# Group norm statistics made one layer early, and a convolution shared out anew between TensorE and VectorE

## The chip, the cores and the metric

The kernel runs on one core of one Trainium2 chip. The metric is device time in microseconds, from one execution's start to its end; a time of the kernel is the median of several executions. The profile is of one further execution, with its own time. Engines are written as in the profile: PE (TensorE), PEld (its weight loads), DVE (VectorE), ACT (ScalarE), POOL (GpSimd), SP (the queue that issues all DMAs here).

## The reference

Four images of 64 x 64 pixels with 192 channels pass through four layers. Each layer is a residual block: group norm over 32 groups of 6 channels and all pixels, then a state space model, added to its input.

```python
def _gn(v, G=32, eps=1e-5):
    B_, H_, W_, C_ = v.shape
    g = v.reshape(B_, H_, W_, G, C_ // G)
    m = jnp.mean(g, axis=(1, 2, 4), keepdims=True)
    s = jnp.var(g, axis=(1, 2, 4), keepdims=True)
    return ((g - m) / jnp.sqrt(s + eps)).reshape(v.shape)

x = x + _L0_conv_ref(_gn(x), ...)   # a: four directions, rows and columns, 4-tap convolution along each, 384 channels
x = x + _L1_conv_ref(_gn(x), ...)   # b: 3x3 depthwise convolution, one snake-wise direction, 384 channels
x = x + _L2_conv_ref(_gn(x), ...)   # c: 3x3 depthwise convolution, four directions, 192 channels
x = x + _L3_conv_ref(_gn(x), ...)   # d: as c, 384 channels
```

Inside a layer (here b), with 16 states per channel:

```python
xc, z = jnp.split(x @ in_proj_w.T, 2, axis=-1)
xc = silu(conv(xc) + conv_b)
dts, Bs, Cs = split(x_proj_w @ xc)
delta = softplus(dt_w @ dts + dt_b)
h[t] = exp(delta[t] * A) * h[t-1] + delta[t] * xc[t] * B[t]     # along the direction
y[t] = sum over states of h[t] * C[t]  +  D * xc[t]
y = layer_norm(y) * silu(z)                                     # a: without the layer norm
out = y @ out_proj_w.T
```

## The kernel before

`net` (L936) goes image by image and layer by layer. An image of a layer is 192 channels by 4096 pixels, kept as two halves (`k`) of 96 partitions; between layers it lies in DRAM, and a layer writes it in eight chunks of 512 pixels (8 image rows). Every layer has three stages, each with its own pools of tiles in SBUF and PSUM (`p1`, `p2`, `p3`).

**First stage (p1).** `load_x` (L65) reads the layer's input in four DMAs of 1024 pixels. `stats` (L83) sums all pixels on DVE (L87), multiplies the sums with `gmat` on PE to get the group's mean (L89), squares the distances on ACT in eight pieces with accumulated sums (L99), and makes the reciprocal root from a second small matmul (L106) with `rsqrt` (L72: Ln and Exp on ACT, then a Newton step on DVE). `normalize` (L113) then writes x in place in two instructions of 96x4096.

For b, c and d, `conv` (L123) follows. The inner channels are `nb` blocks of `P` (three of 128; in c two of 96). The weights `wu` and the taps `cp` are issued on SP at L130 and L132, after x. For each block, in the order 1, 2, 0, there are eight projections into PSUM (`pu`, L150, two matmuls each; the profile shows two records for each matmul) and eight copies by ACT into the padded image `pad` (L154). Blocks other than 0 are convolved on DVE: nine taps, one instruction each over the whole block of 4096 elements (L160 the first, L162 the other eight), then a silu on ACT (L137; in b two instructions, L138 and L139, since odd rows are turned round). Block 0 is convolved on PE: for each of eight chunks nine matmuls with a diagonal matrix of taps (`diag` L168, `pc` L177), and a silu.

For a, `conv1d` (L185) is called for each of four directions, with three blocks each: projections (L210), copies (L214), four taps on DVE (L238 and L240), silu (L241) into `xo`, and a DMA of `xo` to DRAM (L242). Block 0's first 16 rows (`CONV_ROWS`) go by PE (L232, L233) instead. `pad` has four buffers, `xo` two.

**Scans (p2).** `scans` (L269) handles tiles of 128x1024: decays by ACT, inflow on POOL or as transposes on PE, the scan on DVE, outflow on DVE or POOL, sums on PE. The order on each engine is written out by hand: `keep` (L256) ties every instruction to the one before it on its engine. In layer a (`short`) the start of each row must not carry a state over, so some decays are written into three fixed tiles that POOL sets to zero beforehand (L293), leaving each row's first column alone.

**Output (p3).** `output` (L680) reads the directions' results in eight chunks, adds them, makes layer norm statistics per pixel (L705, L706), gates by silu of a second projection; then for eight chunks it normalizes (L727), transposes (L734), scales (L744), multiplies (L745), projects (L752), adds the layer's input (`gy`, L747) into `res` on DVE (L756, once per half) and stores it (L757). Layer a has `out0` (L802), whose `finish` (L836) does the same last steps at L839 and L842.

**Order.** Outside the scans a planner in the language's framework orders each engine's instructions when the kernel is built, by program order and by when it thinks their inputs are ready. In the profile, `dg` (L168) runs before the mean is copied (L91), for example, and taps of two blocks take turns on DVE. Engines then work through their lists in order. `behind` (L56) forces a few places. A new stage's pools take over the memory of the old one's: in the profile, the first load and the first memset of a first stage begin when the last store of the stage ahead has landed.

Of the kernel before, what the change touches and what calls it, by code (L numbers as in the profile page):

```python
# [7 lines left out]
F32 = mybir.dt.float32  # L8
AF = mybir.ActivationFunctionType
ALU = mybir.AluOpType  # L10
# [17 lines left out]
CONV_ROWS = 16  # L28
POOL_SHORT = 5, 8
# [15 lines left out]
class Net:  # L45
    def __init__(self, tc, d, const):
        self.tc, self.nc, self.d = tc, tc.nc, d
        self.pinned = {}
        nc = self.nc
        self.ident = const.tile([128, 128], F32, tag="ident", name="ident")  # L50
        make_identity(nc, self.ident)
        self.gmat = const.tile([HP, HP], F32, tag="gmat", name="gmat")
        nc.sync.dma_start(self.gmat, d["gmat"])
# [11 lines left out]
    def load_x(self, pool, x_src, key):  # L65
        x = pool.tile([HP, 2, L], F32, tag="x", name=f"x_{key}")
        for q in range(4):
            s = slice(q * (L // 4), (q + 1) * (L // 4))
            self.nc.sync.dma_start(x[:, :, s], x_src[:, :, s])
        return x  # L70
# [12 lines left out]
    def stats(self, keep, pool, pp, x, key):  # L83

        nc = self.nc
        sums = pool.tile([HP, 2], F32, tag="sums", name=f"sums_{key}")
        nc.vector.tensor_reduce(sums, x, AX.X, ALU.add)  # L87
        ps = pp.tile([HP, 2], F32, tag="gps", bufs=1, name=f"gm_{key}")
        nc.tensor.matmul(ps, self.gmat, sums, start=True, stop=True)  # L89
        mean = keep.tile([HP, 2], F32, tag="mean", name=f"mean_{key}")  # L90
        nc.vector.tensor_copy(mean, ps)  # L91
        neg = pool.tile([HP, 2], F32, tag="neg", name=f"neg_{key}")
        nc.vector.tensor_scalar(neg, mean, -1.0, None, ALU.mult)
        part = pool.tile([HP, 2, 4], F32, tag="part", name=f"part_{key}")
        for k in range(2):
            for q in range(4):
                n = L // 4
                junk = pool.tile([HP, n], F32, tag="junk", bufs=2, name=f"junk_{key}{k}{q}")
                nc.scalar.activation(  # L99
                    junk, x[:, k, q * n : (q + 1) * n], AF.Square, bias=neg[:, k : k + 1],  # L100
                    accum_out=part[:, k, q : q + 1],
                )
        sq = pool.tile([HP, 2], F32, tag="sums", name=f"sq_{key}")
        nc.vector.tensor_reduce(sq, part, AX.X, ALU.add)
        ps = pp.tile([HP, 2], F32, tag="gps", bufs=1, name=f"gv_{key}")
        nc.tensor.matmul(ps, self.gmat, sq, start=True, stop=True)  # L106
# [4 lines left out]
        return mean, rstd  # L111

# [10 lines left out]
    def conv(self, pool, pp, xn, xc, sums, P, nb, w_u, cpack, taps, shape, interior, borders, snake, key):  # L123
# [16 lines left out]


        done = []
        for b in [*range(1, nb), 0]:
# [11 lines left out]
            if b:  # L155
                acc = img(sums[:, b, :])
                for i, (tr, tcol) in enumerate(taps):
                    v = pad[:, tr : tr + H, tcol : tcol + W]
                    if i == 0:
                        nc.vector.tensor_scalar(acc, v, cp[:, b, :1], None, ALU.mult)  # L160
                    else:
                        nc.vector.scalar_tensor_tensor(  # L162
                            acc, v, cp[:, b, i : i + 1], acc, ALU.mult, ALU.add
                        )
                done.append(silu(img(xc[:, b, :]), acc, b))
                continue
# [7 lines left out]
            for ch in range(NCH):  # L174
# [10 lines left out]
    def conv1d(self, pool, pp, xn, out, w_u, cpack, cols, rev, key):  # L185
# [10 lines left out]
        for b in range(nb):  # L196
# [37 lines left out]
            a = img(acc)[:, r0:, :]  # L234
            for i, t in enumerate(taps):
                v = pad[:, t + r0 : t + H, :] if cols else pad[:, r0:, t : t + W]
                if i == 0:
                    nc.vector.tensor_scalar(a, v, cp[:, b, :1], None, ALU.mult)  # L238
                else:
                    nc.vector.scalar_tensor_tensor(a, v, cp[:, b, i : i + 1], a, ALU.mult, ALU.add)  # L240
            done.append(nc.scalar.activation(to[:, r0:, :], a, AF.Silu, bias=bias))  # L241
# [27 lines left out]
    def scans(self, sp, pp, dp, xc, P, nb, dirs, short):  # L269
# [16 lines left out]
        if short:  # L286
# [3 lines left out]
            fixed = []  # L290
            for k in range(3):
                f = sp.tile([P, NT, T], F32, tag=f"dAs{k}", bufs=1, name=f"dAs{k}_{dirs[0][3]}")
                keep(nc.gpsimd.memset(f, 0.0))  # L293
                fixed.append(f)
# [205 lines left out]
        def decay(t):  # L500
# [3 lines left out]
            elif short:  # L504
                t.dA = fixed[t.turn % 3]
# [174 lines left out]
    def output(self, pool, pp, P, nb, outs, wz, wo, ln, snake, x_src, norm, dst, key):  # L680
# [8 lines left out]
        for ch in range(NCH):  # L689
# [21 lines left out]
            for b in range(nb):  # L711
# [5 lines left out]
                gates.append(nc.scalar.activation(z[:, b, s], pz, AF.Silu))  # L717
        v = pool.tile([128, NCH * TB, 1], F32, tag="v", name=f"v_{key}")
# [4 lines left out]
        for ch in range(NCH):  # L723
# [33 lines left out]
            nc.sync.dma_start(dst[:, :, s], res)  # L757

    def layer0(self, x_src, dst, dp):
        tc, nc, d = self.tc, self.nc, self.d
        P, nb = 128, 3
        with tc.tile_pool(name="a_keep", bufs=1) as keep:
            jobs = []
            with tc.tile_pool(name="a_p1", bufs=1) as pool, tc.tile_pool(
                name="a_p1ps", bufs=1, space=PSUM
            ) as pp:
                x = self.load_x(pool, x_src, "a")
                nc.scalar.preload_act_table_set(NLE)  # L770
                norm = self.stats(keep, pool, pp, x, "a")
                self.normalize(x, x, norm)
# [24 lines left out]
            with tc.tile_pool(name="a_p3", bufs=1) as pool, tc.tile_pool(  # L797
                name="a_p3ps", bufs=1, space=PSUM
            ) as pp:
                self.out0(pool, pp, x_src, norm, [j[4] for j in jobs], dst)  # L800

    def out0(self, pool, pp, x_src, norm, outs, dst):  # L802
# [32 lines left out]

        def finish(ch, x, po):  # L836
# [5 lines left out]
            nc.sync.dma_start(dst[:, :, ch * T : (ch + 1) * T], res)  # L842

# [34 lines left out]
        finish(late[0], late[4], late[3])  # L878

    def layer(self, name, x_src, dst, dp, P, nb, dirs, snake, twice):  # L880
# [5 lines left out]
        with tc.tile_pool(name=f"{name}_keep", bufs=1) as keep:  # L886
            with tc.tile_pool(name=f"{name}_xc", bufs=1) as xp:
                xc = xp.tile([P, nb, L], F32, tag="xc", name=f"xc_{name}")
                with tc.tile_pool(name=f"{name}_p1", bufs=1) as pool, tc.tile_pool(
# [3 lines left out]
                    x = self.load_x(pool, x_src, name)  # L893
                    nc.scalar.preload_act_table_set(NLE)
                    norm = self.stats(keep, pool, pp, x, name)
# [133 lines left out]
```

## Time and profile before

| | us |
|---|---|
| median of 3 runs | 35065.01 (35061.34 to 35067.1) |
| the profiled execution | 35048.62 |
| its span, first to last instruction | 35046.5 |

| engine | busy us | share of the span |
|---|---|---|
| PE | 25072.0 | 72% |
| PEld | 18264.5 | 52% |
| DVE | 27941.2 | 80% |
| ACT | 23687.5 | 68% |
| POOL | 25888.4 | 74% |

DMA moved 98 GB/s over the span; the mean granted clock of PE was 0.810. The four images take nearly the same time each (a, b, c and d in turn): the second image's layer a begins to load at 8759.65 us.

A line of a timeline gives start, duration, engine, line of the code, operation, what it writes and reads, shapes, the count, and in brackets how long the engine stood idle before and what released it. A line of waits gives who waited, for whom, then the sum in us, how often, and the longest. "Idle before" matters only on the engine that is late.

### The profile page before, as it was taken

Reading aid. Unit: us, or ns where it says so; the run is one execution under the profiler, and the core shown is the slowest. Engines: PE = TensorE matmul, PEld = TensorE weight load, DVE = VectorE, ACT = ScalarE, POOL = GpSimd, SP = SyncE. Lnnn points to the kernel's source line nnn. Section 1 sums busy time; section 2 is a strip of 40 time slices with the busy share of each in tenths; the row PEclk is TensorE's granted clock in tenths of the full one; section 3 lists DMA queues with packets and bytes.
Section 4 is the critical chain, followed back from the end, with each engine's and each line's share of the span. In section 5 each row is a group of like instructions: output and inputs, shape, how many; then the busy total and the mean of one; then the engine's idle time right before and its main releaser. Section 6 shows DMA issues by size and latency. Waiting matters only on the chain. (4 is left out here: it accounts for less than half of the span.)

```text
span 35046.5 us, 390536 instructions
## 1 busy us (share of the span) xinstructions
PE 25072.0 (72%) x135744; PEld 18264.5 (52%) x135744; DVE 27941.2 (80%) x22892; ACT 23687.5 (68%) x44483; POOL 25888.4 (74%) x11298
## 2 busy tenths in 40 slices
PE   7778777766777877776677787777667778777766
PEld 4554454554455445455445544545544554454554
DVE  7885797887788579788778857978877885797887
ACT  6773585776677358577667735857766773585776
POOL 6882696887588269688758826968876882696887
PEclk8888777878888887788888888778788888777878
DMA  3332233223333223322333322332233332233223
GB/s 107 106 106 76 85 106 98 94 94 110 107 106 106 75 86 106 98 93 93 111 106 106 107 75 86 108 97 94 94 111 106 106 106 76 85 106 98 94 94 111
DMA packets 1370822, 3443.13 MB, mean 98 GB/s; under 512 B 183201, under 2 KB 630545, under 8 KB 1362705
## 3 DMA queue, kind: packets, MB, share of 16 engines
q1 hardware_dynamic: 1368848, 3418.15, 31.1%
q8 instruction: 1076, 17.63, 0.2%
q14 instruction: 898, 7.35, 0.1%
HBM read 2962.60 MB, written 455.08 MB: 98 GB/s over the span
## 5 line engine op out<-in xcount | busy, mean ns | idle before, releaser
L595 PE MATMUL py_d<-ident,c_d 128*128 128x128 f32 x24576 | 3815.0, 314 | 2143.3 <-POOL c_d L577 1313.4
L595 PE MATMUL py_a<-ident,c_a 128*128 128x128 f32 x24576 | 3630.7, 302 | 2217.6 <-POOL c_a L577 1149.3
L577 POOL TENSOR_TENSOR c_d<-h_d,C_d 128x1024 f32<-128x1024 f32 x2036 | 4779.0, 2368 | 162.5 <-DVE h_d L560 159.9
L577 POOL TENSOR_TENSOR c_a<-h_a,C_a 128x1024 f32<-128x1024 f32 x1908 | 4479.4, 2371 | 414.8 <-issue 281.3
L595 PEld LDWEIGHTS py_d<-ident,c_d 128*128 128x128 f32 x24576 | 3359.8, 164 | 2596.2 <-POOL c_d L577 1633.4
L595 PEld LDWEIGHTS py_a<-ident,c_a 128*128 128x128 f32 x24576 | 3150.5, 156 | 2527.0 <-DVE c_a L577 1267.2
L522 POOL TENSOR_TENSOR u_d<-du_d,B_d 128x1024 f32<-128x1024 f32 x1536 | 3621.5, 2362 | 899.9 <-issue 886.7
L522 POOL TENSOR_TENSOR u_a<-du_a,B_a 128x1024 f32<-128x1024 f32 x1536 | 3607.4, 2364 | 715.0 <-DVE h_a L553 695.3
L577 POOL TENSOR_TENSOR c_c<-h_c,C_c 96x1024 f32<-96x1024 f32 x1356 | 3179.0, 2361 | 365.4 <-DVE h_c L560 346.2
L560 DVE TENSOR_TENSOR_SCAN h_d<-dA_d,carry_d,u_d 128x512 f32<-128x512 f32 x2536 | 3073.4, 1264 | 334.8 <-POOL c_d L577 264.3
L514 ACT ACTIVATE dA_d<-delta_d,A_d 128x512 f32<-128x512 f32 x3072 | 2118.0, 690 | 1637.0 <-DVE c_d L577 1491.6
L514 ACT ACTIVATE dA_a<-delta_a,A_a 128x512 f32<-128x512 f32 x3072 | 2119.6, 690 | 1243.0 <-DVE c_a L577 1089.6
L595 PE MATMUL py_c<-ident,c_c 96*128 96x96 f32 x16384 | 2232.5, 303 | 865.3 <-DVE c_c L577 653.7
L553 DVE TENSOR_TENSOR_SCAN h_a<-dA_a,u_a 128x1024 f32<-128x1024 f32 x1140 | 2579.4, 2281 | 331.2 <-ACT dA_a L518 178.3
L595 PEld LDWEIGHTS py_c<-ident,c_c 96*128 96x128 f32 x16384 | 2022.9, 180 | 1200.2 <-DVE c_c L577 779.3
L522 POOL TENSOR_TENSOR u_c<-du_c,B_c 96x1024 f32<-96x1024 f32 x1024 | 2412.8, 2362 | 6.3 <-DVE dA_c L560 6.0
L539 PE MATMUL ut_d<-ident,dut_d 128*128 128x128 f32 x12288 | 1911.8, 307 | 620.7 <-DVE c_d L577 595.3
L531 ACT ACTIVATE dut_a<-duT_a,BT_a 128x384 f32<-128x384 f32 x4096 | 2291.2, 604 | 0.0
L531 ACT ACTIVATE dut_d<-duT_d,BT_d 128x384 f32<-128x384 f32 x4096 | 2290.8, 601 | 0.0
L560 DVE TENSOR_TENSOR_SCAN ut_d<-dAs_d,carry_d,ut_d 128x512 f32<-128x512 f32 x1536 | 1971.1, 1283 | 388.3 <-issue 166.8
L514 ACT ACTIVATE dAs_d<-delta_d,A_d 128x512 f32<-128x512 f32 x3072 | 2042.9, 713 | 295.7 <-DVE h_d L560 230.5
L539 PEld LDWEIGHTS ut_d<-ident,dut_d 128*128 128x128 f32 x12288 | 1587.0, 158 | 1141.8 <-issue 934.9
(356 smaller groups left out, 63171.0 us busy)
## 6 DMA issues: line engine op xcount, KB each, us to landing
C_a<-bc_a SPq DMA_DIRECT2D x1024, 512.0 KB
C_d<-bc_d SPq DMA_DIRECT2D x1024, 512.0 KB
C_c<-bc_c SPq DMA_DIRECT2D x1024, 384.0 KB
B_a<-bc_a SPq DMA_DIRECT2D x512, 512.0 KB
B_d<-bc_d SPq DMA_DIRECT2D x512, 512.0 KB
B_c<-bc_c SPq DMA_DIRECT2D x512, 384.0 KB
C_b<-bc_b SPq DMA_DIRECT2D x256, 512.0 KB
xd_a<-xo_a SPq DMA_DIRECT2D x48, 2048.0 KB
```

The costliest lines, as they stand in the source:

```text
L514: keep(nc.scalar.activation(out, delta, AF.Exp, scale=o.A[:, t.b, k : k + 1]))
L522: keep(nc.gpsimd.tensor_tensor(t.u, t.c.du[:, t.b, None, :].to_broadcast([P, NT, T]), t.c.B[t.j], ALU.mult))
L531: keep(nc.scalar.activation(c.scaled[n][:, q, :], c.duT[:, q, :], AF.Copy, scale=c.BT[:, q, n : n + 1]))
L539: keep(nc.tensor.transpose(t.u[:, n, q * 128 : (q + 1) * 128], t.c.scaled[t.n0 + n][:, q, t.b * P : (t.b + 1) * P], self.ident,))
L553: keep(nc.vector.tensor_tensor_scan(hf, af, uf, 0.0, ALU.mult, ALU.add))
L560: keep(nc.vector.tensor_tensor_scan(hf, af, uf, o.carry[:, t.b, k : k + 1], ALU.mult, ALU.add))
L577: keep(engine.tensor_tensor(t.cm, t.h, t.c.C[t.j], ALU.mult))
L595: keep(nc.tensor.matmul(c.py[b][:, q, :], t.cm[:, n, q * 128 : (q + 1) * 128], self.ident[:P, :P], start=first, stop=c.sums[b] == NS and q ...
```

## The change

1. `moments` makes the statistics of one chunk with `bn_stats`, two instructions per chunk (one for each half), in the output stage: after each chunk's `res` is made, from `res`. In layer d the next input is the next image, so each chunk of it is loaded (`nx`) and read there; after the last image there is none, and `res` is read. The first image's statistics are made ahead of everything from eight loads of their own.
2. `stats` starts from those: `bn_aggr` for each half, mean by a matmul with `gmat`, then each channel's variance plus its squared distance from the group's mean, and a second matmul.
3. `load_normal` loads x in eight DMAs of 512 pixels, and normalizes in sixteen instructions of 96x512.
4. In `conv`, blocks other than 0 are convolved on DVE in two parts (31 and 33 rows; in b 30 and 34), each with its own silu. Block 0's last two chunks (in c its last three) go from PE to DVE.
5. In `conv1d`, DVE's taps and the silu are made in two parts, parted at row 37.
6. Layer a's scans have three fixed tiles for each of the two senses of direction (six memsets for three).

```diff
+CONV_SPLIT = 37
...
-    def load_x(self, pool, x_src, key):
-        x = pool.tile([HP, 2, L], F32, tag="x", name=f"x_{key}")
-        for q in range(4):
-            s = slice(q * (L // 4), (q + 1) * (L // 4))
-            self.nc.sync.dma_start(x[:, :, s], x_src[:, :, s])
-        return x
+    def moments(self, st, x, ch):
+
+        for k in range(2):
+            self.nc.vector.bn_stats(st[:, k, ch, :], x[:, k, :])
+
+    def new_moments(self, key):
+        return self.const.tile([HP, 2, NCH, 6], F32, tag="mom", bufs=2, name=f"mom_{key}")
...
-    def stats(self, keep, pool, pp, x, key):
+    def stats(self, keep, pool, pp, st, key):
 
         nc = self.nc
-        sums = pool.tile([HP, 2], F32, tag="sums", name=f"sums_{key}")
-        nc.vector.tensor_reduce(sums, x, AX.X, ALU.add)
+        mv = pool.tile([HP, 2, 2], F32, tag="gmv", name=f"gmv_{key}")
+        for k in range(2):
+            nc.vector.bn_aggr(mv[:, k, :], st[:, k, :, :])
         ps = pp.tile([HP, 2], F32, tag="gps", bufs=1, name=f"gm_{key}")
-        nc.tensor.matmul(ps, self.gmat, sums, start=True, stop=True)
+        nc.tensor.matmul(ps, self.gmat, mv[:, :, 0], start=True, stop=True)
         mean = keep.tile([HP, 2], F32, tag="mean", name=f"mean_{key}")
         nc.vector.tensor_copy(mean, ps)
-        neg = pool.tile([HP, 2], F32, tag="neg", name=f"neg_{key}")
-        nc.vector.tensor_scalar(neg, mean, -1.0, None, ALU.mult)
-        part = pool.tile([HP, 2, 4], F32, tag="part", name=f"part_{key}")
-        for k in range(2):
-            for q in range(4):
-                n = L // 4
-                junk = pool.tile([HP, n], F32, tag="junk", bufs=2, name=f"junk_{key}{k}{q}")
-                nc.scalar.activation(
-                    junk, x[:, k, q * n : (q + 1) * n], AF.Square, bias=neg[:, k : k + 1],
-                    accum_out=part[:, k, q : q + 1],
-                )
-        sq = pool.tile([HP, 2], F32, tag="sums", name=f"sq_{key}")
-        nc.vector.tensor_reduce(sq, part, AX.X, ALU.add)
+
+        far = pool.tile([HP, 2], F32, tag="far", name=f"far_{key}")
+        nc.vector.tensor_tensor(far, mv[:, :, 0], mean, ALU.subtract)
+        nc.vector.tensor_tensor(far, far, far, ALU.mult)
+        nc.vector.tensor_tensor(far, far, mv[:, :, 1], ALU.add)
         ps = pp.tile([HP, 2], F32, tag="gps", bufs=1, name=f"gv_{key}")
-        nc.tensor.matmul(ps, self.gmat, sq, start=True, stop=True)
+        nc.tensor.matmul(ps, self.gmat, far, start=True, stop=True)
...
+    def load_normal(self, pool, x_src, norm, key):
+        x = pool.tile([HP, 2, L], F32, tag="x", name=f"x_{key}")
+        for ch in range(NCH):
+            s = slice(ch * T, (ch + 1) * T)
+            self.nc.sync.dma_start(x[:, :, s], x_src[:, :, s])
+        for ch in range(NCH):
+            s = slice(ch * T, (ch + 1) * T)
+            self.normalize(x[:, :, s], x[:, :, s], norm)
+        return x
...
+        def on_vector(b, pad, lo, hi):
+            acc = img(sums[:, b, :])[:, lo:hi, :]
+            for i, (tr, tcol) in enumerate(taps):
+                v = pad[:, tr + lo : tr + hi, tcol : tcol + W]
+                if i == 0:
+                    nc.vector.tensor_scalar(acc, v, cp[:, b, :1], None, ALU.mult)
+                else:
+                    nc.vector.scalar_tensor_tensor(
+                        acc, v, cp[:, b, i : i + 1], acc, ALU.mult, ALU.add
+                    )
+            done.append(silu(img(xc[:, b, :])[:, lo:hi, :], acc, b))
...
             if b:
-                acc = img(sums[:, b, :])
...
+                half = H // 2 - 1 - snake
+                on_vector(b, pad, 0, half)
+                on_vector(b, pad, half, H)
                 continue
...
-            for ch in range(NCH):
+            own = 6 if nb > 2 else 5
+            on_vector(b, pad, own * R, H)
+            for ch in range(own):
                 pc = pp.tile([P, T], F32, tag="pc", bufs=3, name=f"pc_{key}{ch}")
...
-            a = img(acc)[:, r0:, :]
-            for i, t in enumerate(taps):
-                v = pad[:, t + r0 : t + H, :] if cols else pad[:, r0:, t : t + W]
...
-            done.append(nc.scalar.activation(to[:, r0:, :], a, AF.Silu, bias=bias))
+
+            for lo, hi in ((r0, CONV_SPLIT), (CONV_SPLIT, H)):
+                a = img(acc)[:, lo:hi, :]
+                for i, t in enumerate(taps):
+                    v = pad[:, t + lo : t + hi, :] if cols else pad[:, lo:hi, t : t + W]
...
+                done.append(nc.scalar.activation(to[:, lo:hi, :], a, AF.Silu, bias=bias))
...
-            fixed = []
-            for k in range(3):
-                f = sp.tile([P, NT, T], F32, tag=f"dAs{k}", bufs=1, name=f"dAs{k}_{dirs[0][3]}")
-                keep(nc.gpsimd.memset(f, 0.0))
-                fixed.append(f)
+
+            fixed = {}
+            for rev in sorted({job[2] for job in dirs}):
+                fixed[rev] = []
+                for k in range(3):
+                    f = sp.tile([P, NT, T], F32, tag=f"dAs{rev}{k}", bufs=1, name=f"dAs{rev}{k}_a")
+                    keep(nc.gpsimd.memset(f, 0.0))
+                    fixed[rev].append(f)
...
-                t.dA = fixed[t.turn % 3]
+                t.dA = fixed[o.rev][t.turn % 3]
...
             nc.sync.dma_start(dst[:, :, s], res)
+            if x_next is None:
+                self.moments(st, res, ch)
+            else:
+                x = pool.tile([HP, 2, T], F32, tag="nx", bufs=2, name=f"nx_{k}")
+                nc.sync.dma_start(x, x_next[:, :, s])
+                self.moments(st, x, ch)
+        return st
...
-                x = self.load_x(pool, x_src, "a")
                 nc.scalar.preload_act_table_set(NLE)
-                norm = self.stats(keep, pool, pp, x, "a")
-                self.normalize(x, x, norm)
+                norm = self.stats(keep, pool, pp, st, "a")
+                x = self.load_normal(pool, x_src, norm, "a")
...
             nc.sync.dma_start(dst[:, :, ch * T : (ch + 1) * T], res)
+            self.moments(st, res, ch)
...
+        st = n.new_moments("x")
+        with tc.tile_pool(name="first", bufs=1) as pool:
+            for ch in range(NCH):
+                x = pool.tile([HP, 2, T], F32, tag="x", bufs=4, name=f"x0_{ch}")
+                tc.nc.sync.dma_start(x, halves(d["x"][0])[:, :, ch * T : (ch + 1) * T])
+                n.moments(st, x, ch)
...
-        "gmat": ((group[:, None] == group[None, :]) / (6.0 * L)).astype(np.float32),
+        "gmat": ((group[:, None] == group[None, :]) / 6.0).astype(np.float32),
```

## The prediction

> **What bounds the kernel now.** I cut the first image into stages with busy time per window (each row: stretch, length, then busy time and instruction count of PE, weight loads, DVE, ACT and POOL, granted TensorE clock, DMA share, GB/s). Layer a's scans, its output stage, then layer b's first stage and its scans:
>
> ```profile
> 290.00:2715.00 2425.00, 1711.99 (x10874) 1371.21 (x10874) 2076.37 (x1065) 1891.51 (x3396) 2114.55 (x897) 0.84 0.33 106
> 2715.00:3106.00 391.00, 385.32 (x1200) 186.06 (x1200) 85.68 (x128) 62.41 (x109) 0.00 (x0) 0.99 0.29 86
> 3106.00:3260.00 154.00, 108.36 (x245) 47.48 (x246) 91.34 (x30) 43.17 (x66) 1.37 (x12) 0.84 0.10 26
> 3260.00:3907.00 647.00, 442.87 (x2720) 362.39 (x2718) 553.04 (x520) 467.30 (x878) 540.84 (x231) 0.81 0.27 89
> ```
>
> The scans are 7159 of the first image's 9043 us (2425 + 647 + 1593 + 2494, the same cut for all four layers), held by DVE and POOL at 85 to 92%. The change leaves their code and pinned order alone, apart from three memsets. What it touches is the first stage (290, 154, 141 and 154 us for a, b, c, d: 739 per image) and the output stages (391, 139, 132, 197). In a first stage no engine is busy throughout, so I read layer b's by its timeline:
>
> ```profile
> 3105.00 0.75 DVE L839 SCALAR_TENSOR_TENSOR gr_a<-po_a,fcb_a,gx_a 96x512 f32<-96x512 f32 x1 [1.83 <-PE po_a L831]
> 3123.50 8.68 DVE L87 TENSOR_REDUCE sums_b<-x_b 96x2 f32<-96x8192 f32 x1 [17.76 <-DMA x_b<-x]
> 3146.88 4.73 DVE L116 TENSOR_SCALAR x_b<-x_b,mean_b,rstd_b 96x4096 f32<-96x4096 f32 x2
> 3167.95 2.35 DVE L160 TENSOR_SCALAR cs_b<-pad_b,cp_b 128x4096 f32<-128x4096 f32 x1 [16.34 <-ACT pad_b L154]
> 3186.11 57.60 DVE L162 SCALAR_TENSOR_TENSOR cs_b<-pad_b,cp_b,cs_b 128x4096 f32<-128x4096 f32 x13
> ...
> 3151.66 43.02 PE L150 MATMUL pu_b<-x_b,wu_b 96*128 96x512 f32 x94 [0.25 <-DVE x_b L116]
> 3194.53 61.97 PE L177 MATMUL pc_b<-pad_b,dg_b 128*128 128x512 f32 x144
> ...
> 3256.91 0.47 ACT L139 ACTIVATE xc_b<-pc_b,cp_b 128x256 f32<-128x256 f32 x1
> ```
>
> The reader is to see one chain: last output row 3105.75, input landed 3123.50, sums, squares and normalization until 3151.6, projections, then 72 convolution matmuls (144 records) on PE until 3256.5, last silu 3257.38. DVE is through at 3243.7. The chain is 151.6 us. Two records precede the 94, so at full pace the projections begin at 3151.66 - 0.86 = 3150.8. The same reading gives, for input landed / projections / last silu: c 4063.95 / 4090.95 / 4184.56, d 5930.2 / 5957.5 / 6063.45, second image's a 8775.2 / 8802.4 / 9032.4 (there the last silu is of DVE's last block).
>
> **Statistics off the path.** Between landing and projections lie sums 8.68, mean and negation about 1.7, eight squares 9.2, second sum to rstd 3.8, and normalization: 27.3 us in b, 27.0 to 27.3 elsewhere. All of it goes behind the load. The new statistics need two aggregates, two small matmuls with their copies, the two table loads and Newton's step; from rows of the same work (gm to neg 1.3, sq to rstd 3.8, aggregates 0.16 each) this is some 6 us. They use tiles of the new pools, which open only when the last store has landed: memset and load both began at 3109.0. So rstd is there at about 3115 and the 16 normalizations of 96x512 (0.53 each in the output stage) keep up with pieces that land every 1.5 us. The wait for the input stays, and so does one that the old statistics covered: the weights wu are issued behind x on SP.
>
> ```profile
> SPq L309 <- DMA x_b<-x: 10.9, 1, 10.9
> SPq L69 <- DMA x<-gr_a: 2.5, 1, 2.5
> SPq L309 <- DMA wu_b<-in_b_in: 0.9, 1, 0.9
> ```
>
> SP's later waits, in total and longest us: after x_b it still waited 0.9 us for wu_b, so the two land in order, wu at about 3124.4. The first projection needs wu, thus everything starts there: x landed + 0.9 (c's wu is half as large: 0.5). Gain at the head: b 27.3 - 0.9 = 26.4, c 26.5, d 26.4, a 26.3. In the first image's layer a the input is read once for the statistics (landed near 17 us) and again afterwards; the second load follows the last bn_stats, so projections start near 18 + 15.4 + 1 = 34 us against 42: 8 only.
>
> **Eight pieces for four.** Here a rule speaks against the change. While output stages store and load 384 KB pieces, windows of 1 us show
>
> ```profile
> 4008.00:4009.00 1.00, 0.26 (x2) 0.24 (x2) 0.00 (x0) 1.00 (x4) 1.00 (x2) 1.00 0.97 231
> 4009.00:4010.00 1.00, 1.00 (x3) 0.33 (x2) 0.00 (x0) 1.00 (x3) 1.00 (x2) 1.00 0.91 326
> ```
>
> that is 0.79 MB in about 2.8 us, as fast as the 262 GB/s at which x_b came in 768 KB pieces. The Trainium skill ("DMA: Bandwidth & Descriptors", section "Bandwidth") wants transfers of 1 MiB or more and calls smaller ones inefficient; with its fit of 2.0 us plus bytes at 436 GB/s, pieces one after the other would cost 8 x 2.9 = 23 us instead of 4 x 3.8 = 15: an estimate of 8 us per layer, 128 in all. The row has pieces in flight together, so I take nothing. SP's eight issues of about 0.55 us (4.4) lie inside 12 us of transfer.
>
> **Convolution in b and d.** PE loses two of eight chunks: 12.6 to 15.5 us, here 2 x 7.73. DVE gains rows 48 to 64 of block 0: one tap at 0.65 and eight at 1.25, 10.6 us (3072 against 4096 elements gives 1.04 ns per element; steps within a run add 0.16 to 0.25 us). Halving blocks 1 and 2 doubles 18 instructions, 0.2 us each. DVE's sum is 75.8 + 3.5 + 10.6 = 90. It may begin when four chunks are copied, 10.2 us after the projections begin (ACT's fourth copy), not 17.1. It ends at 10.2 + 90 = 100, plus 1 to 3 us of silu: 101.6. PE is done at 43.8 + 6 x 7.73 = 90: DVE becomes the end. Before: 106.6 in b, 105.9 in d. Gain 5.0 and 4.3.
>
> **Convolution in c.** PE: 30.9 of projections + 5 x 7.73 = 69.5, + 0.7 silu = 70.2. DVE: 11.1 + 39.6 + 15.1 (24 rows) = 66, just under it. Before 93.6: gain 23.4, the largest single one.
>
> **Layer a.** PE's work is unchanged (12 projections at 13.8, four times 7.0 of taps, 2.7 of slow first matmuls: 196). DVE's 178 us get 36 more tap instructions of about 0.2: 186. Splitting at row 37 lets DVE start after five chunks. Followed block by block with these durations, the last block ends 210 us after the projections begin instead of 222.7; silu of 27 rows then costs 3.1 where 64 cost 7.2. That would be 213.5 against 230, a gain of 16.5; but ACT's in-order silus held back copies for some 8 us in the old trace (DVE's 9.68 us before its last two blocks). Between 8 (these holds stay) and 16.5 (they go) I take 12.
>
> **Costs.** A bn_stats of 128x384 took 0.54, so 96x512 about 0.65, two per chunk 1.3. In layer a's output stage they fit between the second gr (ends 3019.25) and the next go (3020.84); DVE idles 4 us and more per chunk in b and d; in c three chunks meet DVE's early backlog: 2 us. Uncovered they would cost 1.3 x 8 x 16 = 166. Layer d's extra loads queue on SP behind a store, ahead of the next gy: each waits for the bn_stats two chunks back, long done; DMA is 0.61 busy there. Three more memsets of 0.95 on POOL end at about 9045.5, before POOL's next work at 9052.8: nothing, at most 2.9 per layer a.
>
> **Sum.** Per image a 38.3, b 31.4, c 47.9, d 30.7 = 148.3; times four 593, less 18 for the first image: 575. The profiled run took 35048.62 (span 35046.5); 35049 - 575 = 34474. The runs' median, 35065.01, is 16 above it: 34490, or 1.6% less.
>
> **Rivals.** *Weights first* (34363): if wu is ahead of x in SP's queue, projections start with the first piece, rstd setting them at about 3116: 8.5 us x 15 more, 127. The old order x, wu, cp in all four layers speaks against. *Convolution gives nothing back* (34669): only the heads gain, since DVE parts end late or copies are held; 44.7 x 4 = 179 less. For it: DVE is already the end in a and becomes so in b and d; against: c's is a PE saving with room. *ACT in program order* (35258, slower): if a block's copies are queued behind the preceding block's two silus, projections stall until DVE is done; per image I get 56 each in b and d, 30 in c, 50 in a, 192, times four 768 more than forecast. It decides above 144 us per image (575 / 4). Against: in b all 24 copies precede the first silu now, so the order already follows readiness; and in a, copies that stand between silus bring no table load with them.
>
> **How the numbers follow.** Forecast 0.69 (own range 34420 to 34560: the holds in a 8 x 4, b and d 3 x 8, landing 2 x 16), weights first 0.13, nothing back 0.14, ACT order 0.04. The range 34340 to 34620 leaves out the last two, 0.18. No change means within 0.2%, about what a measurement of this kernel can tell; only ACT order, or a milder form of it, reaches there: faster 0.95, same 0.01, slower 0.04.
>
> **What would show it.** Right: first projections about 1 us behind x, near 19 us after the last gr; L177 records in b 108 instead of 144; DVE the last to end in b and d, PE in c; first stages of some 248, 123, 91 and 123 us for a to d; scans unchanged. Wrong: projections starting piece by piece, PE idle for copies inside the projections, go_a later in a's output stage, or scans that differ.

## The result and the profile after

The changed kernel takes **34511.69 us** (median of 4 runs, 34507.41 to 34518.72) against 35066.06 (35061.34 to 35071.43) for the kernel before beside it: a ratio of 0.9842, 95% interval 0.9825 to 0.9859, or 1.6% less. The forecast was 34490 with a range of 34340 to 34620. The profiled execution took 34507.41, its span is 34505.6; the span of before was 35046.5, so the two traces differ by 540.9 us, where the sum of the prediction had 575.

To see where they lie I cut both traces at the same five instructions of each of the 16 layers: the last output row (gr) of the layer ahead, the first projection (pu), the last silu of the first stage, the first matmul of the scans (px), the first of the output stage. "First stage" is from the last gr ahead to the last silu. In us, before to after, for one layer of each kind and as a sum over all four images:

| layer | to first projection | projection to last silu | first stage, gained per layer | predicted |
|---|---|---|---|---|
| a, images 2 to 4 | 44.5 to 19.4 | 231.5 to 230.8 | 25.8, 25.9, 25.6 | 38.3 |
| a, first image | 40.5 to 32.3 | 230.3 to 230.0 | 8.5 | 20 |
| b | 43.6 to 18.7 | 108.0 to 101.0 | 31.9, 32.6, 32.6, 33.2 | 31.4 |
| c | 44.0 to 17.8 | 95.1 to 69.6 | 51.7, 51.6, 48.8, 51.5 | 49.9 (47.9 with its output stage) |
| d | 43.5 to 18.9 | 107.4 to 105.3 | 26.7, 28.6, 30.3, 29.7 | 30.7 |

The first stages gave 535.1 us together (heads 390.7, convolutions 144.4), scans and output stages with the steps between them 5.9: the sums of the scans and of the output stages changed by +44.1 and -48.0, which is the cut between them moving, since the first matmul of the output stage comes later.

The windows of the four stages that the prediction began with, cut again in the changed kernel (stretch, length, busy time and instruction count of PE, weight loads, DVE, ACT and POOL, granted TensorE clock, DMA share, GB/s):

```profile
282.00:2700.00 2418.00, 1715.80 (x10874) 1372.70 (x10874) 2076.25 (x1065) 1891.31 (x3396) 2114.69 (x897) 0.84 0.32 105
2700.00:3097.00 397.00, 383.12 (x1200) 183.83 (x1200) 95.98 (x143) 62.62 (x110) 0.00 (x0) 0.98 0.30 88
3097.00:3217.00 120.00, 91.90 (x208) 40.58 (x208) 99.97 (x75) 33.38 (x52) 1.29 (x12) 0.88 0.13 32
3217.00:3882.00 665.00, 450.01 (x2721) 370.46 (x2722) 556.24 (x530) 468.44 (x879) 540.94 (x231) 0.79 0.28 91
```

DVE's work in the scans of a is the same to 0.2 us (2076.37 then, 2076.25 now). In a's output stage DVE has about 10 us more, the bn_stats; the window is 6 us longer only because it was cut earlier, by the marks of the table's cuts the stage is 2.8 us shorter (386.4 against 389.2). In b's first stage PE has fallen from 108 to 92 us and DVE has risen from 91 to 100 of 120.

Layer b by its timeline (start, duration, engine, line, output from inputs, count, the idle time before and what ended it):

```profile
3096.31 0.75 DVE L868 SCALAR_TENSOR_TENSOR gr_a<-po_a,fcb_a,gx_a 96x512 f32<-96x512 f32 x1 [1.10 <-PE po_a L858]
3097.09 0.69 DVE L69 BATCH_NORM_STATS2 mom_a<-gr_a 96x6 f32<-96x512 f32 x1
3100.25 0.60 DVE L90 BATCH_NORM_AGGREGATE gmv_b<-mom_a 96x2 f32<-96x48 f32 x2 [2.47 <-DMA x<-gr_a]
3100.32 3.76 SPq L112 DMA_DIRECT2D x_b<-x  x8
3104.16 0.41 SPq L135 DMA_DIRECT2D wu_b<-in_b_in  x1
3106.89 4.65 DVE L121 TENSOR_SCALAR x_b<-x_b,mean_b,rstd_b 96x512 f32<-96x512 f32 x10
...
3114.65 1.00 DVE L121 TENSOR_SCALAR x_b<-x_b,mean_b,rstd_b 96x512 f32<-96x512 f32 x2 [0.48 <-DMA x_b<-x]
3115.79 44.61 PE L169 MATMUL pu_b<-x_b,wu_b 96*128 96x512 f32 x96 [12.98 <-DVE x_b L121]
...
3197.91 17.46 DVE L155 SCALAR_TENSOR_TENSOR cs_b<-pad_b,cp_b,cs_b 128x2176 f32<-128x2176 f32 x11
3215.41 0.72 ACT L143 ACTIVATE xc_b<-cs_b,cp_b 128x512 f32<-128x512 f32 x1 [4.78 <-DVE cs_b L155]
3216.04 0.70 ACT L144 ACTIVATE xc_b<-cs_b,cp_b 128x512 f32<-128x512 f32 x1
```

The reader is to see that rstd is there at 3106.9, that five chunks are normalized in one go, and that PE begins only at 3115.79, once the last piece of x and, behind it in SP's queue, wu have landed. The end is now DVE's taps and one silu of 16 rows. In d and in the later a the trace names wu itself as what ended PE's wait:

```profile
5835.69 4.61 PE L169 MATMUL pu_d<-x_d,wu_d 96*128 96x512 f32 x5 [13.36 <-DMA wu_d<-in_d_in]
8652.78 16.86 PE L225 MATMUL pu_a<-x_a,wu_a 96*128 96x512 f32 x32 [13.84 <-DMA wu_a<-in_a_in]
```

So three layers of four came out within 2 us of the sum on average, and layer a gave a third less than predicted: its convolution, from the first projection to the last silu, is as long as it was. That is what most of the experiments are about.

### The profile page after: what moved, and what is told of

It is laid out like the page before. It is cut to its first block, busy times and chain, and to the rows that moved or that the text cites. A ratio compares the mean times of both kernels' runs of the same rounds, so it can differ in the third digit from the quotient of the medians.

```text
span 34505.6 us, 390569 instructions
## 1 busy us (share of the span) xinstructions
PE 24862.7 (72%) x135240; PEld 18214.6 (53%) x135240; DVE 28332.2 (82%) x23900; ACT 23542.8 (68%) x44285; POOL 25842.7 (75%) x11310
```

## The experiments

Totals of one kernel differ between occasions: the changed kernel came out at 34512 once and at 34501 another time. A difference in totals of some 25 us is therefore read from the stages of the trace, where a layer's first stage repeats within 1 to 3 us. Each ratio is against runs of the kernel before on the same occasion.

### Even rows in every part

Layer a's groups in the changed kernel's trace show the suspect. DVE's first tap (L255, by shape: busy us, mean ns of one), in its second image:

```profile
L255 DVE TENSOR_SCALAR acc_a<-pad_a,cp_a 128x1728 f32<-128x1728 f32 x12 | 18.7, 1562 | 2.5 <-ACT pad_a L229 2.5
L255 DVE TENSOR_SCALAR acc_a<-pad_a,cp_a 128x2368 f32<-128x2368 f32 x8 | 16.5, 2064 | 19.3 <-ACT pad_a L229 19.3
L255 DVE TENSOR_SCALAR acc_a<-pad_a,cp_a 128x1344 f32<-128x1344 f32 x4 | 5.0, 1262 | 10.6 <-ACT pad_a L229 10.6
```

and in the kernel before, in the same layer:

```profile
L238 DVE TENSOR_SCALAR acc_a<-pad_a,cp_a 128x4096 f32<-128x4096 f32 x8 | 18.8, 2351 | 28.5 <-ACT pad_a L214 28.5
L238 DVE TENSOR_SCALAR acc_a<-pad_a,cp_a 128x3072 f32<-128x3072 f32 x4 | 7.3, 1816 | 16.8 <-ACT pad_a L214 16.8
```

Together 26.1 us before and 40.2 now, for the same rows. The means of the changed kernel mix two kinds: in directions 0 and 1 the parts of 21, 27 and 37 rows take 1.61, 2.01 and 2.68 us, in directions 2 and 3 0.91, 1.11 and 1.45, so the number of elements alone is not the cause. Before, the parts of 48 and 64 rows took 1.82 and 2.35 in all four. In the row directions a row of the padded tile is 64 of 70 elements; in the column directions the rows shifted over lie one behind the other without a gap.

```diff
-CONV_SPLIT = 37
+CONV_SPLIT = 36
...
-                half = H // 2 - 1 - snake
+                half = H // 2 - 2
```

> The changed kernel with every tap part on an even number of rows: layer a split at row 36 instead of 37, the halves of b, c and d of 30 and 34 rows (30 instead of 30 or 31). Theory (the first tap of a part loses its fast mode where the row count is odd and the rows are strided): the first taps of c and d fall from 2.27 and 2.40 us to about 1.22 and 1.35, those of a's two row directions from 1.61, 2.01 and 2.68 to about 0.90, 1.13 and 1.45. Layer d is then 4.2 us shorter (DVE ends it), c unchanged (PE ends it), a 8 to 12 shorter if DVE sets it: 34455 us in all (34445 to 34465). Rival (a is held by ACT's in-order silus, not by DVE's work): a moves by less than 3, 34495 in all.

Measured: 34452.38 us (34446.08 to 34460.21), ratio 0.9825, 0.981 to 0.984. Layer a's convolution fell to 221.5, 220.9, 221.1 and 221.1 (by 8.5, 9.8, 9.7 and 9.8), d's by 2.8 to 4.7, b's and c's by 0.1 to 1.6. The same groups in this trace:

```profile
L255 DVE TENSOR_SCALAR acc_a<-pad_a,cp_a 128x1792 f32<-128x1792 f32 x12 | 13.8, 1148 | 2.9 <-ACT pad_a L229 2.9
L255 DVE TENSOR_SCALAR acc_a<-pad_a,cp_a 128x2304 f32<-128x2304 f32 x8 | 11.3, 1418 | 21.2 <-ACT pad_a L229 21.2
L255 DVE TENSOR_SCALAR acc_a<-pad_a,cp_a 128x1280 f32<-128x1280 f32 x4 | 3.5, 880 | 10.4 <-ACT pad_a L229 10.4
```

The first taps take 28.6 us instead of 40.2, with the same rows in all: 11.6 us of DVE per layer a. A part of 1792 elements is now quicker than one of 1728 was. The rival, that ACT alone holds layer a, would have left a where it was; it falls. It gained 9.5, inside the 8 to 12 expected of this run and short of the 12 that the prediction had for the change. The waits in layer a say what else is in it. What ACT and PE waited for, in the same layer of three kernels (sum in us, how often, the longest): before,

```profile
ACT xo_a L241 <- DVE acc_a L240: 29.7, 11, 8.3
...
PE pu_a L210 <- ACT pad_a L214: 3.7, 1, 3.7
```

the changed kernel,

```profile
ACT xo_a L258 <- DVE acc_a L257: 64.5, 19, 6.8
...
PE pu_a L225 <- DMA wu_a<-in_a_in: 13.8, 1, 13.8
PE pu_a L225 <- ACT pad_a L229: 7.0, 6, 2.1
```

and with even rows

```profile
ACT xo_a L258 <- DVE acc_a L257: 26.4, 20, 5.2
```

With odd parts DVE is late so often that ACT stands 64.5 us in front of silus whose taps aren't done. Copies of projections are queued behind those silus, and PE stands still for 7.0 us because its PSUM tiles aren't copied out. With even rows ACT's waits for taps are below those of before, and PE waits for copies only 0.5 us.

### The cut at row 38 instead of 36

The even cut also lies one row earlier, so that DVE may begin sooner. Here it lies one row later, and b, c and d keep their odd halves.

```diff
-CONV_SPLIT = 37
+CONV_SPLIT = 38
```

> The changed kernel with layer a split at row 38 in place of 37, everything else as it is: parts of 22, 26, 38 and 26 rows, an even number again, but the cut moved the other way than in the run with even rows. Theory (the odd number of rows is what layer a lost by): its convolution takes about 221 us as with the cut at 36, d's stays at 104 to 105, the whole 4 x 9 shorter than the changed kernel, 34470 us. Rival (an earlier cut is what helped): layer a at 231 or more, 34510 or above.

Measured: 34487.29 us (34483.48 to 34491.84), ratio 0.9834, 0.9817 to 0.985. Layer a's convolution takes 223.9, 223.4, 223.6 and 223.7: 6.1, 7.3, 7.2 and 7.1 below the changed kernel; d stays at 104.8 to 105.0. So an even number of rows is worth at least 7 of the 9.5 us, since this cut lies a row later than the changed kernel's. The two even cuts, two rows apart, differ by 2.5; halfway between them the rows would be worth about 8 (an estimate from these two runs). The total is 17 above what I expected, of which the smaller gain explains 8.

### What decides: the number of rows or the row that a part starts with

```diff
-                half = H // 2 - 1 - snake
-                on_vector(b, pad, 0, half)
-                on_vector(b, pad, half, H)
+                cuts = (0, 31, 61, H) if nb == 2 else (0, H // 2 - 1 - snake, H)
+                for lo, hi in zip(cuts, cuts[1:]):
+                    on_vector(b, pad, lo, hi)
```

> The changed kernel with layer c's VectorE block in three parts: rows 0 to 31, 31 to 61 and 61 to 64, that is an even start with 31 rows, an odd start with 30 rows, and an odd start with 3 rows. Theory (the number of rows decides): the first tap of 0 to 31 takes 2.27 us, that of 31 to 61 1.22, that of 61 to 64 the slow pace, about 0.26. Rival (the start row decides): 31 to 61 takes about 2.2 us. The other taps take 2.21 us for 30 rows in either case. The total hardly moves, 34512 + 5.

Measured: 34458.14 us in one run. Layer c's first taps in its timeline:

```profile
4037.20 2.27 DVE L153 TENSOR_SCALAR cs_c<-pad_c,cp_c 96x1984 f32<-96x1984 f32 x1 [8.78 <-ACT pad_c L173]
4046.41 1.21 DVE L153 TENSOR_SCALAR cs_c<-pad_c,cp_c 96x1920 f32<-96x1920 f32 x1
4069.17 0.40 DVE L153 TENSOR_SCALAR cs_c<-pad_c,cp_c 96x192 f32<-96x192 f32 x1
```

Rows 0 to 31 (even start, 31 rows) 2.27 us; rows 31 to 61 (odd start, 30 rows) 1.21. The changed kernel and the run with even rows have the other two cases in layer c: 33 rows from an odd start 2.40, 30 rows from an even start 1.22. The number of rows decides, the start doesn't. The three rows took 0.40 where I expected 0.26. That is the time of a later tap of the same shape (0.41), as 2.27 at 31 rows is (2.28): with an odd number of rows the first tap loses the whole of its lead over the others. This one total of 54 below the changed kernel lies in scans and output stages, whose code is the same, and I draw nothing from a single run.

### Silus behind the next block's copies

With even rows ACT still waited 26.4 us for taps in layer a. Here the silus of DVE's parts are held back until the eight copies of the block after have been issued, across directions too.

```diff
-                nc.scalar.copy(inside[:, ch * R : (ch + 1) * R, :], rows(pu))
+                last = nc.scalar.copy(inside[:, ch * R : (ch + 1) * R, :], rows(pu))
+            self.flush([last])      # the held silus, behind that copy, and xo's store
...
-                done.append(nc.scalar.activation(to[:, lo:hi, :], a, AF.Silu, bias=bias))
-            nc.sync.dma_start(out[:, b, :], xo)
+                self.held.append((to[:, lo:hi, :], a, bias, out[:, b, :], xo, done))
```

> The kernel with even rows, and in layer a the silus of VectorE's parts put behind the eight copies of the block after, so that ScalarE never waits for taps while copies are ready. Theory (the holds that are left in a cost PE its stalls): layer a's convolution falls from 221 to about 208 (199 us of PE plus the last part), 34452 - 50 = 34400 us. Rival (what is left in a is the order of PE's own work and the last part's 11 us, and the silus that move to the end are added there): 34450 to 34470.

Measured, with even rows: 34404.03 us (34401.49 to 34438.15), ratio 0.9817, 0.9802 to 0.9832. Layer a's convolution takes 214.0, 213.3, 212.8 and 213.0, about 8 less than with even rows alone (13 was expected). The total fell by 48 as expected, but only 31 of it are layer a's convolutions; the rest is scattered over scans and output stages, whose code is the same. All waits of ACT in this layer:

```profile
ACT pad_a L237 <- PE pu_a L233: 89.8, 70, 14.6
ACT xo_a L257 <- PE pc_a L256: 7.8, 4, 2.8
ACT xo_a L203 <- issue: 2.2, 1, 2.2
```

None is for DVE any more. What remains of the layer is PE's work of 195.6 us and 17.6 us behind its last matmul, DVE's last part and its silu.

### Weights ahead of the input

```diff
+                    wu, cp = self.conv_weights(pool, w_in[:, :, :inner], cv, P, nb, 1, name)
                     x = self.load_normal(pool, x_src, norm, name)
```

The loads of wu and cp leave the convolution and stand ahead of x's eight pieces (in layer a those of direction 0).

> The changed kernel with the loads of the first stage's weights (wu, cp; in layer a those of direction 0) issued ahead of the eight pieces of x on SP's queue. Theory (the landing of wu behind x sets the first projection): the first projection starts one normalized piece behind rstd, about 11 us after the last output row instead of 18.7 to 19.5, 7.8 less in 15 layers and some 8 in the first: 34512 - 125 = 34387 us. Rival (the projections wait for the whole of x, whatever wu does, as b's first matmul names the last normalization): the start stays where the last piece lands, a gain below 1 us per layer, 34500 or, with x pushed back by wu's 1.1 us, 34530.

Measured: 34378.18 us (34377.87 to 34385.54), ratio 0.9804, 0.9788 to 0.9821. The first projection starts 10.6 to 11.9 us after the last output row in 15 layers, 6.2 to 8.9 earlier, and 9.0 earlier in the first; heads give 120.5 us in all, and the convolutions pass it on (6.0 us lost over 16 of them). Layer b of this kernel:

```profile
3095.35 0.32 SPq L110 DMA_DIRECT2D wu_b<-in_b_in  x1
3096.22 4.96 SPq L126 DMA_DIRECT2D x_b<-x  x8
3102.88 0.16 DVE L83 TENSOR_TENSOR rstd_b<-rstd_b,rsq_gb 96x2 f32<-96x2 f32 x1
3103.07 1.91 DVE L135 TENSOR_SCALAR x_b<-x_b,mean_b,rstd_b 96x512 f32<-96x512 f32 x4
3103.67 8.52 PE L178 MATMUL pu_b<-x_b,wu_b 96*128 96x512 f32 x13 [5.83 <-DVE x_b L135]
```

PE starts 0.6 us after the first normalization. It is the landing of wu, not of x as a whole, that held the projections: PE needs no more of x than its first piece, so the last normalization, which the trace names as the end of b's wait in the changed kernel, only happened to end as wu landed.

### Each half of the change alone

Statistics and pieces alone (the old convolutions in the changed kernel):

> Part one of the change alone: statistics in the output stage ahead and the input in pieces, with the convolutions of the kernel before. Theory (the parts add up): the heads give their 391 us, the convolutions nothing: 35066 - 391 = 34675 us (34660 to 34690). Rival (the old convolutions profit too, since DVE begins earlier): below 34640. Rival (the heads' gain is partly given back in a first stage that has not been divided): above 34720.

Measured: 34618.29 us (34609.14 to 34629.12), ratio 0.9872, 0.9858 to 0.9887. The heads give 384.8, the convolutions another 24.8, 0.4 to 3.2 in each. Neither rival is needed for it: in the kernel before, two whole-row normalizations stood ahead of the projections, the first matmul needs only the first of them, and so my cut "first projection" there fell some 1.5 us before the point from which PE runs through (in b 3149.34 against 3150.8). Sixteen times 1.5 is 24. The head's true gain is thus about 26.5 us in 15 layers, as predicted. Layer a's convolution is at 228.5 to 230.0 here: with whole blocks it is 1.2 us shorter on average than divided at row 37.

The divided convolutions alone (in the kernel before):

> The other part alone: the kernel before with the divided taps and the rows moved to VectorE. Theory (the parts add up): b 7, c 25, d 2 to 5 and a 0.7 less per layer, 144 us in all: 35066 - 144 = 34922 us (34905 to 34940). Rival (part of the loss in a comes only with the early start of the projections): a gives its 12 here, 34875.

Measured: 34948.37 us (34923.12 to 34954.46), ratio 0.9965, 0.9952 to 0.9978. b gives 5.7 to 7.0, c 21.6 to 23.9, d 1.0 to 3.5, and a loses 0.5 to 2.3. The sum is 122.6, that is 144 less 22, about what the cut accounts for. The two halves add up, 448 + 117 = 565 against 554 for both. Dividing layer a at an odd row is a small loss with the old head and with the new one.

### More bn_stats than needed

Every bn_stats twice, and then five times, the surplus into a tile that nobody reads:

```diff
+            spare = self.const.tile([HP, 6], F32, tag="spare", bufs=2, name=f"spare_{st.name}{k}{ch}")
+            self.nc.vector.bn_stats(spare, x[:, k, :])
             self.nc.vector.bn_stats(st[:, k, ch, :], x[:, k, :])
```

> The changed kernel with every bn_stats of the output stages done twice, the second time into a tile that nobody reads: 1.4 us of DVE more per chunk, 8 chunks in 16 layers (179 us of work). Theory (it lies in DVE's idle time): a b and d output stage unchanged, the last chunk's 1.4 us partly seen in the head behind it (up to 0.7 per layer), c's some 2 us longer: 34512 + 8 to 20 = 34525 us. Rival (VectorE's time counts in the output stages, so the change itself pays 179 us for its statistics): 34690.

Measured: 34487.01 us (34483.53 to 34490.94), ratio 0.9838, 0.9822 to 0.9855; not slower, but 25 less than the changed kernel. Its stages: 7.0 us more in the first image's head, where nothing covers the eight chunks, all other heads within 1.6 of the changed kernel's, and the rest spread over scans and output stages. To learn whether the 25 us mean anything, the changed kernel ran once more.

> The changed kernel once more, unaltered, as the measure of the run with bn_stats twice, which came out 25 us faster than the changed kernel's record. Theory (those 25 us are what two runs on different occasions differ by): 34485 to 34500 beside it here. Rival (a second bn_stats does something good): 34512 again.

Measured: 34500.87 us (34494.53 to 34504.5), ratio 0.9843, 0.9829 to 0.9858. That is between the two expectations; 14 of the 25 us remain, which I cannot place and do not explain. What is shown is that 179 us of added DVE work cost nothing that could be measured, apart from some 7 us in the first image's head.

> Every bn_stats of the output stages five times, four of them into a tile that nobody reads: 5.5 us more of DVE per chunk, 707 us of work in 16 layers. Theory (cover of a finite size): in a's output stage a chunk takes 45 us of PE and DVE's gates come every 3.7 us, so most of 5.5 us is now seen there, up to 5 x 8 x 4 = 160; b and d have 4 us of idle per chunk, c none, together about 100 to 200; the heads 5.5 x 15 = 80 more. In all 34512 + 250 to 450, about 34850. Rival (VectorE's queue has room for all): 34600, the heads alone.

Measured: 34700.61 us (34689.36 to 34711.46), ratio 0.9902, 0.9885 to 0.9918: 707 us of work, 189 of them seen. The cover does end, but not where I expected: a's output stages hide everything (-2.2 to +0.6 us), b's grow by 9 to 15, c's by 15 to 19, d's by 3 to 12, and the heads by 53, of which 36 in the first image's.

### Together

Weights first, even rows, and the table of Ln and Exp loaded right behind the output stage's last silu, so that the statistics find it:

```diff
+        self.load_table(gates)      # preload behind the last silus; Ln is put behind it
         with self.behind(gates):
             self.rsqrt(pool, r, v, [128, NCH * TB, 1], key)
```

> Weights first and even rows together, and the table of Ln and Exp loaded once, right behind the output stage's last silu, where the chain of the statistics now loads two tables of 1.28 us. Theory (three separate terms on the path, which add up): 34512 - 60 - 133 = 34319 us without the tables; with them 2.6 us less per head in 15 layers, 34280 us, and down to 34250 if the output stages of b, c and d gain theirs too. Rival (the first projection waits for a piece of x by then, not for rstd): 34319.

Measured: 34293.8 us (34272.9 to 34300.5), ratio 0.9782, 0.9768 to 0.9797. The heads are at 8.9 to 10.2 us, 1.6 below those with weights first alone, not 2.6. Layer b shows why:

```profile
3089.07 0.20 ACT L83 ACTIVATE rsq_gb<-v_b 96x2 f32<-96x2 f32 x1 [15.59 <-DVE v_b L108]
3089.30 0.20 ACT L84 ACTIVATE rstd_b<-rsq_gb 96x2 f32<-96x2 f32 x1
3090.12 0.16 DVE L88 TENSOR_TENSOR rstd_b<-rstd_b,rsq_gb 96x2 f32<-96x2 f32 x1
3090.20 1.35 DVE L195 TENSOR_TENSOR dg_b<-ident,cp_b 128x1152 f32<-128x1152 f32 x1
3092.05 1.00 DVE L140 TENSOR_SCALAR x_b<-x_b,mean_b,rstd_b 96x512 f32<-96x512 f32 x2 [0.50 <-DMA x_b<-x]
```

No table load stands between Ln and Exp any more, and rstd is there at 3090.28, but DVE then waits for the first piece of x until 3092.05. The diagonal matrices (`dg`) that slipped in ahead of it were done 0.5 us earlier and cost nothing here. The rival named for this run holds for about 1 us of the 2.6.

With the late silus as well:

> The same with the late silus in layer a as well. Theory: the difference between the runs with and without late silus is the same as at the old head, -50 us, 34230 us. Rival: no gain or a loss of up to 20, 34280 to 34300.

Measured: **34267.76 us** (34258.3 to 34277.4), ratio 0.9776, 0.9761 to 0.979, the fastest of all. Layer a's convolution is at 213.1 to 213.5, 7.8 less on average than in the run above, so late silus are worth the same with the new head as with the old; the total fell by 26, half of what was expected, where the convolutions show 35, with output stages that came out 20 longer.

## Why the prediction was right, and the step that failed

**The bound and what is left alone**: right. Scans and output stages changed by 5.9 us of some 32100, as much as they differ between two traces of the changed kernel (5.8).

**Statistics off the path**: right in size and in mechanism. First projections were to begin near 19 us after the last output row and began at 17.3 to 19.5 in 15 layers; rstd was to be there some 6 us into its chain and took 6.6 (3100.25 to 3106.86 in b). That wu, behind x on SP, becomes the limit was the reading of one line of SP's waits, and the run with weights first shows it. That run also realizes the rival of that name: 34363 worked out, 34378 measured. As an account of this change it is excluded, for the changed kernel's order is x, wu, cp.

**Eight pieces for four**: right to take nothing. In b the pieces of x were issued from 3100.32 and the last was being normalized at 3114.65, 14.3 us; before, 3109.0 to 3123.50, 14.5. The 8 us per layer that the prediction worked out from the rule of one MiB are not there.

**Convolution in b and c**: right. From the start of projections b's last silu was to come at 101.6 and came at 101.0, with DVE last; L192 has the 108 records. c: 70.2 against 69.6, with PE last. c's gain of 51 us per layer with its head is the largest, as said.

**Layer a, and in part d, failed**: the step was "DVE's 178 us get 36 more tap instructions of about 0.2: 186". DVE had 194.3 us of work in the window of the second image's layer a, and 182.1 with even rows. The change makes 48 more tap instructions there, not 36. Thirty-six are second or later taps; their sum rose from 148.6 to 156.2 us, which is the 0.2 each that was set down. The other twelve are first taps, which the sum left out, and the first taps rose by 14.1 us, from 26.1 to 40.2; with even rows they rose by 2.5. So the term that failed is the first taps, put at nothing: what half of one costs was taken to be half of the whole. Before, every part had 48 or 64 rows, so no line of that profile could show what an odd number does. The Trainium skill does: "VectorE: DVE Perf Modes", section "What auto-detection actually checks", lets a single-source operation stream two elements per cycle where the outermost dimensions of source and destination, leaving out those of length one, are both even or equal. A part of 31 rows reads 31 rows of 64 with gaps and writes 1984 elements without any. If rows that touch count as one run, 31 and 1984 are neither; that they do so is my reading, and no run tests it by itself. The runs agree to the row: 2.27 us for 31, 1.21 for 30 at an odd start, and no loss in the column directions, where source and destination are both without gaps. They agree in the pace too: between 21 and 37 rows a first tap takes 1.04 ns per element in the row directions and 0.52 in the column directions. This was the rule that spoke against the change, and I weighed another.

The size of the miss follows, here for the second image. The 12 us in a were taken between 8, if ACT's holds stay, and 16.5, if they go, from a start at full pace, which in the kernel before lies 1.5 us behind the first projection of the table (8802.4 against 8800.95). From there a's convolution took 230.0 before, and 230.8 as changed: no gain but a loss of 0.8. With even rows, where ACT still waits 26.4 us for taps, it is 220.9, a gain of 9.1; with the silus moved as well it is 213.3, where the block-by-block reading had 213.5. Both ends of the bracket come out for parts with even rows, but the upper one only with an edit that the change does not have. With odd rows DVE's 11.6 us more made it late, ACT's waits for taps doubled from 29.7 to 64.5, and the copies behind them stopped PE for 7.0 where it had been 3.7. That is one of the signs of being wrong that the prediction named, PE idle for copies inside the projections, and a mild form of the rival *ACT in program order*, in a alone. In d the odd halves cost 4.0 us per layer, more than the 1.9 by which d fell short.

Of the lengths foretold for the first stages, counted up to the first matmul of the scans, b's 123 (122) and c's 91 (89) hold, d's 123 (126) is 3 short, and a's 248 (264) is 16 short. Layer a's own step explains 12.6 of these; the rest is that 248 came from a window that ends at 9043, 3.8 us ahead of the first such matmul in the kernel before (9046.8).

**The sum**: a 49 us short in all (12.6 in each of the last three, 11.5 in the first), d 7.5 short, b 4.8 and c 4.0 over, and 13.9 from scans and output stages, where 8 us were set aside for bn_stats in c and 5.9 were gained instead: -34, from 575 to 541. That the total came so near the forecast is in part luck: a and d are 57 us short between them, and 22.7 us on the other side, most of them not foretold, make up for part of it. The bn_stats were longer than estimated, 0.69 instead of 0.65 us, and hidden; so were the aggregates, 0.30 each instead of 0.16.

**The other rivals**: *Convolution gives nothing back* is excluded for b and c by 7 and 25 us per layer, and holds for layer a as the change divides it. No run has the two edits of b, c and d, the division and the rows moved from PE to DVE, each by itself. In c PE ends the stage before and after; it is through 68.9 us after the first projection instead of 94.4, and the three chunks taken from it, 7.73 each, are 23.2 of these 25.5.

## What to carry to other kernels

When an operation is cut into parts, price a part by a row of the same shape, and if the trace has none, ask what the part's shape changes besides its length; an even cut was worth 51 us in the first stages here (59 in the total) for the cost of changing two constants. When a stall is taken off the path, look at what is issued last into the queue behind it: eight pieces of input ahead of one small weight load gave away 115 us in the first stages (133 in the total). And where an in-order engine serves two others, the slower of these stops the faster one through it: ACT's waits for DVE were the first sign of PE's.

## What the runs showed of the hardware that I had not expected

A TENSOR_SCALAR over rows with gaps takes 2.27 us for 31 rows of 64 and 1.21 for 30; one row more nearly doubles it, to the time of a tap that reads two tensors. Those, the second tap and all after it, show no such step: 2.21 us for 30 rows against 2.28 for 31.

DVE's room in the output stages is larger than I had thought: 11 us of additional bn_stats in each of them left no trace in the times, and 44 us in each stage of layer a, where I expected most to be seen, left none either.
